# The last graph of a two-layer graph network emitted by halves of its nodes

## The chip, the cores and the metric

The kernel runs on one core of one Trainium2 chip. The metric is the device time of one execution in microseconds (us). A run's time is compared as the median of several executions. The profile is of one further execution; its times are counted from the first instruction (the span), and it has a time of its own.

## What is computed

There are 64 graphs of 256 nodes with 256 features each, and for each a 256x256 adjacency. Layer 0 is a gated recurrent cell over a convolution along the nodes and messages between them; layer 1 is a graph convolution with a residual. Each layer ends in a layer norm. Cut to what matters here:

```python
x_conv = relu(bn(conv1d(relu(bn(conv1d(x, conv1_w))), conv2_w)) + x)    # along the nodes
x_nmp  = (exp(-dist(x @ w_se.T)) * adj) @ relu(x @ w_msg.T + b_msg)
gi, gh = concat(x_conv, x_nmp) @ w_ih.T + b_ih,  x @ w_hh.T + b_hh
r, z   = sigmoid(gi_r + gh_r), sigmoid(gi_z + gh_z)
n      = tanh(gi_n + r * gh_n)
x      = layernorm(x + (1 - z) * n + z * x)
h      = layernorm(x) * ln_gamma + ln_beta
x      = layernorm(x + x + relu((adj @ h) @ W_rel + b_rel + h @ W_root))
```

Layer 0 can be taken graph by graph and node by node once the convolution and the messages are there; layer 1 mixes the nodes of one graph in `adj @ h`.

## The kernel before

**The work.** Graphs are taken in order, `k` = 0 to 63, in eight blocks of eight. A tile of one graph has 128 partitions and two halves: nodes 0 to 127 and 128 to 255 (index `n`). The convolution of the block to come is worked out in small steps, between the parts of the graphs of the present block (`pump`, L940). In the last block there is no convolution to come, so only the graphs' own work is left.

**One graph.** It goes through these functions:

- `gates_rz(k, n)` (L704): for one half, six products of 512 columns into one PSUM bank (L711, L713); VectorE adds the bias (L716) and ScalarE takes the tanh that stands for both sigmoids (L717).
- `gates_n(k, n)` (L719): products for the third gate (L723, L725) and their bias (L726).
- `update(k)` (L733), in three steps. First, for both halves at once: two operations on VectorE into `nn` and its tanh on ScalarE (L739). Second: three operations on VectorE into `w` (L743 and two recorded at the helper's line L103), the statistics of each half (`stats`, L730 and L731), and on GpSimd the two reciprocal roots by a power (L752 to L754) and the shift of the first (L756, L757). Third: `h`, the normalised state, on VectorE (L762), and `X1`, the layer's output, on ScalarE (L765).
- `transposes_h(k)` (L769): `h` is turned by TensorE (L775); ScalarE takes it to `hT` with gamma and beta (L777).
- `project(k)` (L781): for each half two products of 512 columns with `W_rel` and `W_root` side by side (L788); ScalarE copies the first 256 columns to `hr` (L789).
- `aggregate(k)` (L793), in three steps. First: for each half, the adjacency times `hr` is added in PSUM to the root product (L800), and VectorE adds the bias into `y` (L802). Second: relu and residual over both halves (L103), statistics, and the last norm's scale and shift on GpSimd (L810 to L813). Third: ScalarE applies them (L816) and issues the store of both halves (L817).

A product of 512 or of 256 columns is two instructions in the profile, a transpose one: `x8` beside L788 means four products, `x4` beside L775 four transposes.

**The order.** It is written out by hand: each engine runs its instructions in the order in which the program emits them, and waits at the first that is not ready. The loop over `k` (L949 to L990) emits a graph's gates among the second layer of the graph before it: `transposes_h(k - 1)` comes between the gates of the halves, `project(k - 1)` after them, `aggregate(k - 1)` at the end, and the last step of that (the norm's application and the store) after the first gates of the next graph, by `step(y_left)` (L957). After the loop the second layer of graph 63 is emitted alone (L993 to L998): first the last step of graph 62, then graph 63's transposes, projection and aggregation.

**Buffers.** `nn`, `w`, `h`, `hT`, `hr`, `rz` and `gn` have one buffer each, `X1` and `y` two. PSUM's eight banks are handed out in turn. Loads go through SyncE's queue (SP), stores of the output through ScalarE's.

Of the kernel before, what the change touches and what calls it, by code (L numbers as in the profile page):

```python
# [12 lines left out]
F32 = mybir.dt.float32  # L13
AF = mybir.ActivationFunctionType
ALU = mybir.AluOpType

P = 128
B, N, D = 64, 256, 256
C = D // P
TAPS, PAD = 17, 8  # L20
EPS = 1e-5
# [8 lines left out]
BG = 8  # L30
# [45 lines left out]
def gnn_two_layers(  # L76
# [17 lines left out]
    nc = tc.nc  # L94
# [4 lines left out]
    def bank(name):  # L99
        return psum.tile([P, 512], F32, tag="ps", name=name)  # L100

    def stt(o, in0, s, in1, op0=ALU.mult, op1=ALU.add):
        nc.vector.scalar_tensor_tensor(o, in0, s, in1, op0=op0, op1=op1)  # L103
# [25 lines left out]
    mhalf = const.tile([P, 8], F32)  # L129
# [7 lines left out]
    ident = const.tile([P, P], F32)  # L137
# [477 lines left out]
    XG, ADJ, XT, NMP, AT, MSG, X1, H, ST, RZ, OUTS = ({} for _ in range(11))  # L615

    def load(k):

        if k >= B:
            return  # L620
        load_xt(k)
        load_adj(k)
# [9 lines left out]
    def load_x(k):  # L632
        if k < B:
            XG[k] = work.tile([P, C, D], F32, tag="x", name="x")
            nc.sync.dma_start(out=XG[k], in_=x[k].rearrange("(c p) d -> p c d", p=P))
# [51 lines left out]
    def mask(k):  # L687
        nc.vector.tensor_mul(AT[k], AT[k], ADJ[k])

    def passing(k):  # L690
        NMP[k] = work.tile([P, C, N], F32, tag="nmp", name="nmp")
        ps = bank("ps_nmp")
        for d in range(C):
            for m in range(C):
                nc.tensor.matmul(ps[:, d * N:(d + 1) * N], MSG[k][:, m, d * P:(d + 1) * P], AT[k][:, m, :],  # L695
                                 start=(m == 0), stop=(m == C - 1))
        nc.scalar.copy(NMP[k].rearrange("p c n -> p (c n)"), ps)

    def inputs(k, n):
        xc, g = XC[k]  # L700
        q = slice(n * P, (n + 1) * P)
        return q, (xc[:, 0, g, q], xc[:, 1, g, q], NMP[k][:, 0, q], NMP[k][:, 1, q])

    def gates_rz(k, n):  # L704
        if n == 0:
            RZ[k] = (work.tile([P, C, 2 * D], F32, tag="rz", name="rz", bufs=1),
                     work.tile([P, C, 2 * D], F32, tag="gn", name="gn", bufs=1))
        q, ins = inputs(k, n)
        prz = bank("ps_rz")
        for c in range(C):  # L710
            nc.tensor.matmul(prz, XT[k][:, c, q], whh[:, c, 0:2 * D], start=(c == 0), stop=False)  # L711
        for i, t in enumerate(ins):
            nc.tensor.matmul(prz, t, wih[:, i, 0:2 * D], start=False, stop=(i == 3))  # L713
        rz = RZ[k][0]

        nc.vector.tensor_add(rz[:, n, :], prz, brzn[:, :2 * D])  # L716
        nc.scalar.activation(rz[:, n, :], rz[:, n, :], AF.Tanh, scale=0.5)  # L717

    def gates_n(k, n):  # L719
        q, ins = inputs(k, n)  # L720
        pn = bank("ps_n")
        for c in range(C):
            nc.tensor.matmul(pn[:, D:], XT[k][:, c, q], whh[:, c, 2 * D:], start=(c == 0), stop=(c == C - 1))  # L723
        for i, t in enumerate(ins):
            nc.tensor.matmul(pn[:, :D], t, wih[:, i, 2 * D:], start=(i == 0), stop=(i == 3))  # L725
        nc.vector.tensor_add(RZ[k][1][:, n, :], pn, brzn[:, 2 * D:])  # L726

    def stats(mv, k, src):
        st = work.tile([P, 6], F32, tag="bst", name="bst", bufs=4)
        nc.vector.bn_stats(st, src)  # L730
        nc.vector.bn_aggr(mv[:, k, :], st)  # L731
# [37 lines left out]
    def transposes_h(k):  # L769
        hT = work.tile([P, C, N], F32, tag="hT", name="hT", bufs=1)  # L770
        ps = bank("ps_hT")
        for c in range(C):
            for n in range(C):
                q = c * N + n * P
                nc.tensor.transpose(ps[:, q:q + P], H[k][:, n, c * P:(c + 1) * P], ident)  # L775
        for c in range(C):
            nc.scalar.activation(hT[:, c, :], ps[:, c * N:(c + 1) * N], AF.Identity,  # L777
                                 bias=gb[:, 1, c:c + 1], scale=gb[:, 0, c:c + 1])
        H[k] = hT

    def project(k):  # L781
        hT = H[k]
        hr = work.tile([P, C, D], F32, tag="hr", name="hr", bufs=1)
        outs = []
        for n in range(C):
            ps = bank("ps_out")
            for c in range(C):
                nc.tensor.matmul(ps, hT[:, c, n * P:(n + 1) * P], wrr[:, c, :], start=(c == 0), stop=(c == C - 1))  # L788
            nc.scalar.copy(hr[:, n, :], ps[:, :D])  # L789
            outs.append(ps)  # L790
        OUTS[k] = (hr, outs)

    def aggregate(k):  # L793

        hr, outs = OUTS[k]
        y = work.tile([P, C, D], F32, tag="y", name="y")
        for n in range(C):
            po = outs[n][:, D:]
            for m in range(C):
                nc.tensor.matmul(po, ADJ[k][:, m, n * P:(n + 1) * P], hr[:, m, :], start=False, stop=(m == C - 1),  # L800
                                 skip_group_check=True)
            nc.vector.tensor_add(y[:, n, :], po, brel)  # L802
        yield
        stt(y, y, 0.0, X1[k], op0=ALU.max, op1=ALU.add)
        mv = work.tile([P, C, 2], F32, tag="mv", name="mv3", bufs=4)
        for n in range(C):
            stats(mv, n, y[:, n, :])
        q = work.tile([P, C], F32, tag="q3", name="q3", bufs=4)
        sh = work.tile([P, C], F32, tag="sh", name="sh3", bufs=4)
        nc.gpsimd.tensor_scalar(q, mv[:, :, 1], EPS / 4, None, ALU.add)  # L810
        nc.gpsimd.tensor_tensor(q, q, mhalf[:, :C], ALU.pow)
        nc.gpsimd.tensor_mul(sh, mv[:, :, 0], q)
        nc.gpsimd.tensor_scalar(sh, sh, -1.0, None, ALU.mult)  # L813
        yield
        for n in range(C):
            nc.scalar.activation(y[:, n, :], y[:, n, :], AF.Identity, bias=sh[:, n:n + 1], scale=q[:, n:n + 1])  # L816
        nc.scalar.dma_start(out=out[k].rearrange("(c p) d -> p c d", p=P), in_=y)  # L817
        yield


    def step(g):
        if g is not None:
            next(g, None)


    first = conv(0)
    first_pool = ExitStack()
    W2[0] = first_pool.enter_context(tc.tile_pool(name="first", bufs=1)).tile([P, C, NM, D], F32, name="w2all")
    with tc.tile_pool(name="filters", bufs=1, side="right") as filter_pool:
# [47 lines left out]
        brel = const.tile([P, D], F32)  # L877
# [5 lines left out]
        gb = const.tile([P, 2, C], F32)  # L883
# [3 lines left out]
        wrr = const.tile([P, C, 2 * D], F32)  # L887
# [30 lines left out]
    work = ctx.enter_context(tc.tile_pool(name="work", bufs=2))  # L918
# [16 lines left out]
    y_left = None  # L935
    for b in range(NB):
        coming = conv(b + 1) if b + 1 < NB else iter(())
        done, at, goal = 0.0, 0, BG * POINTS - 6

        def pump():  # L940
            nonlocal done, at
            at += 1
            while done < CONV_WEIGHT * at / goal:
                t = next(coming, 1e9)
                if t is None:
                    break
                done += t

        for k in range(b * BG, (b + 1) * BG):  # L949
            load(k + 3)  # L950
            load_x(k + 1)
            up = update(k)
            agg = None
            gates_rz(k, 0)
            pump()
            gates_n(k, 0)
            step(y_left)  # L957
            pump()
            if k > 0:
                transposes_h(k - 1)  # L960
            pump()
            gates_rz(k, 1)
            pump()
            if k + 1 < B:
                passing(k + 1)
            pump()
            if k + 2 < B:
                factors(k + 2)
            gates_n(k, 1)
            pump()  # L970
            if k > 0:
                project(k - 1)
            step(up)
            pump()
            if k + 2 < B:
                distances(k + 2)
            step(up)
            pump()
            if k + 3 < B:
                messages(k + 3)  # L980
            step(up)
            pump()
            if k + 2 < B:
                mask(k + 2)
            if k > 0:
                agg = aggregate(k - 1)
            step(agg)
            step(agg)
            pump()
            y_left = agg  # L990
        for _ in coming:
            pass
    step(y_left)  # L993
    transposes_h(B - 1)
    project(B - 1)
    agg = aggregate(B - 1)
    for _ in range(3):
        step(agg)  # L998

# [40 lines left out]
```

## Time and profile before

| | us |
|---|---|
| median of three runs | 2278.05 (2276.23 to 2279.79) |
| the profiled execution | 2280.43 |
| its span, first to last instruction | 2278.7 |
| TensorE busy in it | 2224.9 |
| VectorE busy | 1678.0 |
| ScalarE busy | 766.9 |
| GpSimd busy | 467.1 |
| mean granted TensorE clock | 0.994 |

In the rows of the timeline the first number is the start in the span and the second the length; a row can hold several instructions in a run, which `x` counts. Square brackets hold the time for which the engine was idle ahead of the row, and what it waited for. Ends of matmuls are modelled. A granted clock of 1.00 is TensorE's full speed. A row can have the line of a helper: all three-operand VectorE work (`stt`) stands at L103, all statistics at L730 and L731.

The tail looks like this. The gates of graph 63 run on TensorE from 2229.70; graph 62's projection starts at 2245.62 and its aggregation at 2249.06, graph 63's transposes at 2255.80, its projection at 2262.45 and its aggregation at 2267.84. The last store is issued at 2275.34.

### The profile page before, as it was taken

The numbers are of one execution on the slowest core, as the hardware profiler recorded it, in microseconds if no ns is written. First come the engines' busy times: TensorE is split into PE (matmuls) and PEld (weight loads), VectorE is DVE, ScalarE is ACT, GpSimd is POOL, SyncE is SP. The second block draws the span as 40 slices with busy tenths as digits, with TensorE's granted clock in tenths as the row PEclk, the third lists the DMA queues.
The fourth block names the chain that finished last, engine by engine and source line by source line (L and its number), as shares of the span: only waits on it lengthen the run. The fifth ranks groups of instructions, "written<-read, shape, count | busy, mean of one in ns | idle before, by whom it ended". The sixth has DMA issues, their size and how long they took to land.

```text
span 2278.7 us, 24459 instructions
## 1 busy us (share of the span) xinstructions
PE 2224.9 (98%) x8386; PEld 1462.9 (64%) x8386; DVE 1678.0 (74%) x3188; ACT 766.9 (34%) x1585; POOL 467.1 (20%) x926
## 2 busy tenths in 40 slices
PE   8999999999999999999999999999999999999996
PEld 5775666666666676656666666666666567666663
DVE  6966889388883998749895698938888398874443
ACT  6433222532234322443224322343223422243332
POOL 0101212122220321223122121222122022122211
PEclk9999999999999999999999999999999999999998
DMA  5931433214422152233422143221442215321100
GB/s 146 314 111 65 139 102 97 97 47 134 139 75 98 57 170 84 75 102 115 140 74 97 62 143 107 95 100 42 139 135 77 98 47 165 98 75 38 46 23 14
DMA packets 212665, 226.68 MB, mean 99 GB/s; under 512 B 22087, under 2 KB 203838, under 8 KB 212542
## 3 DMA queue, kind: packets, MB, share of 16 engines
q1 hardware_dynamic: 189984, 191.14, 26.5%
q10 hardware_dynamic: 22558, 33.99, 4.3%
q8 instruction: 67, 1.10, 0.2%
q14 instruction: 56, 0.46, 0.1%
HBM read 179.22 MB, written 45.88 MB: 99 GB/s over the span
## 4 chain that ended last, share of the span: by engine, by line
PE 76%; DVE 17%; issue 2%; DMA 2%; POOL 1%; ACT 1%; ACTq 0%; SPq 0%; POOLq 0%; DVEq 0%
PE ps_rz L713 16%; PE ps_k L384 10%; PE ps_n L725 8%; PE ps_rz L711 8%; PE ps_out L788 7%; DVE XF L103 6%; PE ps_c L465 5%; PE ps_nmp L695 4%; PE ps_n L723 4%; PE ps_out L800 4%; PE ps_msg L645 4%; DVE w L103 1%; DMA w<-w2m 1%; DVE XF L361 1%; DVE bst L730 1%
## 5 line engine op out<-in xcount | busy, mean ns | idle before, releaser
L103 DVE SCALAR_TENSOR_TENSOR XF<-XF 128x512 f32<-128x512 f32 (+2 forms) x800 | 507.4, 664 | 7.4
L752 POOL TENSOR_SCALAR q<-mv 128x2 f32<-128x2 f32 x64 | 32.1, 501 | 1468.8 <-DVE mv L731 1468.8
L384 PE MATMUL ps_k<-w,XF 128*128 128x256 f32 x1316 | 300.2, 384 | 14.0 <-ACT AT L685 11.6
L384 PEld LDWEIGHTS ps_k<-w,XF 128*128 128x128 f32 x1316 | 247.5, 191 | 61.5 <-ACT AT L685 17.3
L726 DVE TENSOR_TENSOR gn<-ps_n,brzn 128x512 f32<-128x512 f32 x128 | 87.9, 687 | 238.8 <-PE ps_n L725 238.8
L717 ACT ACTIVATE rz<-rz 128x512 f32<-128x512 f32 x128 | 80.6, 630 | 510.7 <-DVE rz L716 510.7
L711 PE MATMUL ps_rz<-whh,xT 128*128 128x512 f32 x512 | 241.8, 595 | 0.0
L713 PE MATMUL ps_rz<-wih,nmp 128*128 128x512 f32 x512 | 240.6, 592 | 0.0
L713 PE MATMUL ps_rz<-wih,xc 128*128 128x512 f32 x512 | 240.6, 592 | 0.0
L788 PE MATMUL ps_out<-wrr,hT 128*128 128x512 f32 x512 | 232.1, 596 | 5.5 <-ACT hT L777 5.5
L716 DVE TENSOR_TENSOR rz<-ps_rz,brzn 128x512 f32<-128x512 f32 x128 | 87.0, 680 | 190.9 <-PE ps_rz L713 190.9
L713 PEld LDWEIGHTS ps_rz<-wih,nmp 128*128 128x128 f32 x512 | 97.3, 190 | 122.4 <-issue 122.4
L713 PEld LDWEIGHTS ps_rz<-wih,xc 128*128 128x128 f32 x512 | 97.3, 190 | 122.4 <-issue 122.2
L788 PEld LDWEIGHTS ps_out<-wrr,hT 128*128 128x128 f32 x512 | 98.0, 192 | 104.7 <-issue 89.1
L656 ACT ACTIVATE msg<-msg 128x512 f32<-128x512 f32 x61 | 38.4, 630 | 332.8 <-DVE msg L654 332.8
L645 PE MATMUL ps_msg<-wms,xT 128*128 128x260 f32 x512 | 131.8, 395 | 4.6 <-DVE XF L400 4.6
L711 PEld LDWEIGHTS ps_rz<-whh,xT 128*128 128x128 f32 x512 | 92.7, 191 | 65.3 <-issue 61.8
L723 PE MATMUL ps_n<-whh,xT 128*128 128x256 f32 x512 | 131.6, 379 | 0.0
L725 PE MATMUL ps_n<-wih,nmp 128*128 128x256 f32 x512 | 131.4, 379 | 0.0
L725 PE MATMUL ps_n<-wih,xc 128*128 128x256 f32 x512 | 131.4, 379 | 0.0
L361 DVE TENSOR_TENSOR XF<-XF 128x512 f32<-128x512 f32 (+3 forms) x128 | 125.2, 1003 | 1.7
L789 ACT COPY hr<-ps_out 128x256 f32<-128x256 f32 x128 | 47.6, 372 | 232.8 <-PE ps_out L788 232.8
(117 smaller groups left out, 3560.5 us busy)
## 6 DMA issues: line engine op xcount, KB each, us to landing
w<-w2m SPq DMA_DIRECT2D x105, 768.0 KB, 5.8
xn<-in_x_dram SPq DMA_DIRECT2D x32, 512.0 KB, 4.4
xt<-xTc ACTq DMA_DIRECT2D x32, 512.0 KB, 3.3
xT<-xt SPq DMA_DIRECT2D x64, 256.0 KB, 3.0
xb<-in_x_dram SPq DMA_DIRECT2D x32, 512.0 KB, 5.9
adj<-in_adjT_dram SPq DMA_DIRECT2D x64, 256.0 KB, 2.8
x<-in_x_dram SPq DMA_DIRECT2D x64, 256.0 KB, 3.0
out_dram<-y ACTq DMA_DIRECT2D x64, 256.0 KB, 2.2
```

The costliest lines, as they stand in the source:

```text
L103: nc.vector.scalar_tensor_tensor(o, in0, s, in1, op0=op0, op1=op1)
L361: (nc.vector.tensor_add if add else nc.vector.tensor_sub)(sl(o, n), sl(a, n), sl(b, n))
L384: nc.tensor.matmul(ps, X[:, slot, c * P:(c + 1) * P], w(m, c), start=(c == 0), stop=(c == C - 1))
L465: nc.tensor.matmul(pss[o], w1[:, c, o * P:(o + 1) * P], xTc[:, c, :], start=(c == 0), stop=(c == C - 1))
L645: nc.tensor.matmul(ps[:, :D + 4], XT[k][:, c, m * P:(m + 1) * P], wms[:, c, :], start=(c == 0), stop=(c == C - 1 and not idle))
L695: nc.tensor.matmul(ps[:, d * N:(d + 1) * N], MSG[k][:, m, d * P:(d + 1) * P], AT[k][:, m, :], start=(m == 0), stop=(m == C - 1))
L711: nc.tensor.matmul(prz, XT[k][:, c, q], whh[:, c, 0:2 * D], start=(c == 0), stop=False)
L713: nc.tensor.matmul(prz, t, wih[:, i, 0:2 * D], start=False, stop=(i == 3))
L723: nc.tensor.matmul(pn[:, D:], XT[k][:, c, q], whh[:, c, 2 * D:], start=(c == 0), stop=(c == C - 1))
L725: nc.tensor.matmul(pn[:, :D], t, wih[:, i, 2 * D:], start=(i == 0), stop=(i == 3))
L788: nc.tensor.matmul(ps, hT[:, c, n * P:(n + 1) * P], wrr[:, c, :], start=(c == 0), stop=(c == C - 1))
L800: nc.tensor.matmul(po, ADJ[k][:, m, n * P:(n + 1) * P], hr[:, m, :], start=False, stop=(m == C - 1), skip_group_check=True)
```

## The change

The loop leaves out graph 63, and a new function `last_graph` emits it. It has the gates of graph 63 and the second layer of graph 62 in it, and everything of graph 63 from `update` on is done for one half at a time, with the halves' steps placed among the steps of graph 62. Graph 62's own second layer keeps its functions. The aggregation of graph 63 runs over `m` (the half that is summed over) in the outer loop and over the output half `n` in the inner one; before, it was the other way round. The last norm is done per half, and each half has its own store: half 0 through SP's queue and half 1 through ScalarE's. All buffers keep their tags and counts, but for the statistics of the last norm, which have a small tag of their own. Instruction shapes become 128x256 (VectorE, ScalarE) and 128x128 (the copies to `hT`), and the GpSimd steps are taken per half on columns of one.

```diff
+    def last_graph(y_before, k):
...
+        def scales(mv, columns):
+
+            q = work.tile([P, 2], F32, tag="q", name="qh", bufs=4)
+            for i, (f, e) in enumerate(columns):
+                nc.gpsimd.tensor_scalar(q[:, i:i + 1], mv[:, 1:2], f, e, ALU.mult, ALU.add)
+            nc.gpsimd.tensor_tensor(q[:, :len(columns)], q[:, :len(columns)], mhalf[:, :len(columns)], ALU.pow)
+            return q
+
+        def shift(mv, q):
+            sh = work.tile([P, 1], F32, tag="sh", name="shh", bufs=4)
+            nc.gpsimd.tensor_mul(sh, mv[:, 0:1], q[:, 0:1])
+            nc.gpsimd.tensor_scalar(sh, sh, -1.0, None, ALU.mult)
+            return sh
+
+        def half(n):
+            rz, gn = RZ[k]
+            a, c = nn[:, n, :], w[:, n, :]
+            stt(a, rz[:, n, :D], 1.0, gn[:, n, D:], op0=ALU.add, op1=ALU.mult)
+            stt(a, a, 0.5, gn[:, n, :D])
+            nc.scalar.activation(a, a, AF.Tanh)
+            yield
+            nc.vector.tensor_sub(c, XG[k][:, n, :], a)
+            stt(c, rz[:, n, D:], 3.0, c, op0=ALU.add, op1=ALU.mult)
+            stt(c, a, 4.0, c)
+            mv = work.tile([P, 1, 2], F32, tag="mv", name="mvh", bufs=4)
+            stats(mv, 0, c)
+            mv = mv[:, 0, :]
+            q = scales(mv, [(1.0, 4 * EPS), (1 + EPS, 4 * EPS * EPS)])
+            nc.vector.tensor_scalar(H[k][:, n, :], c, mv[:, 0:1], q[:, 1:2], ALU.subtract, ALU.mult)
+            sh = shift(mv, q)
+            nc.scalar.activation(X1[k][:, n, :], c, AF.Identity, bias=sh, scale=q[:, 0:1])
+            yield
+
+        def turn_half(n):
+            ps = bank("ps_hT")
+            for c in range(C):
+                nc.tensor.transpose(ps[:, c * P:(c + 1) * P], H[k][:, n, c * P:(c + 1) * P], ident)
+            for c in range(C):
+                nc.scalar.activation(hT[:, c, n * P:(n + 1) * P], ps[:, c * P:(c + 1) * P], AF.Identity,
+                                     bias=gb[:, 1, c:c + 1], scale=gb[:, 0, c:c + 1])
+
+        def project_half(n):
+            ps = bank("ps_out")
+            for c in range(C):
+                nc.tensor.matmul(ps, hT[:, c, n * P:(n + 1) * P], wrr[:, c, :], start=(c == 0), stop=(c == C - 1))
+            nc.scalar.copy(hr[:, n, :], ps[:, :D])
+            outs.append(ps)
+
+        halves_ = [half(n) for n in range(C)]
+        gates_rz(k, 0)
+        gates_n(k, 0)
+        step(y_before)
+        transposes_h(k - 1)
+        step(halves_[0])
+        gates_rz(k, 1)
+        step(halves_[0])
+        gates_n(k, 1)
+        turn_half(0)
+        step(halves_[1])
+        project(k - 1)
+        project_half(0)
+        agg = aggregate(k - 1)
+        step(agg)
+        step(halves_[1])
+        turn_half(1)
+        step(agg)
+        project_half(1)
+        for m in range(C):
+            for n in range(C):
+                nc.tensor.matmul(outs[n][:, D:], ADJ[k][:, m, n * P:(n + 1) * P], hr[:, m, :], start=False,
+                                 stop=(m == C - 1), skip_group_check=True)
+        step(agg)
+        for n in range(C):
+            o = y[:, n, :]
+            nc.vector.tensor_add(o, outs[n][:, D:], brel)
+            stt(o, o, 0.0, X1[k][:, n, :], op0=ALU.max, op1=ALU.add)
+            mv = work.tile([P, 1, 2], F32, tag="mv3", name="mvy", bufs=4)
+            stats(mv, 0, o)
+            q = scales(mv[:, 0, :], [(1.0, EPS / 4)])
+            sh = shift(mv[:, 0, :], q)
+            nc.scalar.activation(o, o, AF.Identity, bias=sh, scale=q[:, 0:1])
+            (nc.sync, nc.scalar)[n].dma_start(out=out[k, n * P:(n + 1) * P, :], in_=o)
...
-        for k in range(b * BG, (b + 1) * BG):
+        for k in range(b * BG, min((b + 1) * BG, B - 1)):
...
-    step(y_left)
-    transposes_h(B - 1)
-    project(B - 1)
-    agg = aggregate(B - 1)
-    for _ in range(3):
-        step(agg)
+    last_graph(y_left, B - 1)
```

More of the change, by code (lines that the diff above doesn't have):

```diff
@@ L823, in step @@
             next(g, None)
+    def last_graph(y_before, k):
+        nn, w, y = (work.tile([P, C, D], F32, tag=t, name=t, bufs=b) for t, b in (("nn", 1), ("w", 1), ("y", 2)))
+        H[k] = work.tile([P, C, D], F32, tag="h", name="h", bufs=1)
+        X1[k] = work.tile([P, C, D], F32, tag="x1", name="x1", bufs=2)
+        hT = work.tile([P, C, N], F32, tag="hT", name="hT", bufs=1)
+        hr = work.tile([P, C, D], F32, tag="hr", name="hr", bufs=1)
+        outs = []
+        def scales(mv, columns):
[74 more added lines that the diff above has]
+            (nc.sync, nc.scalar)[n].dma_start(out=out[k, n * P:(n + 1) * P, :], in_=o)
```

## The prediction

> **What bounds the kernel now.** I read the page first, for the engine that fills the span:
>
> ```profile
> PE 2224.9 (98%) x8386; PEld 1462.9 (64%) x8386; DVE 1678.0 (74%) x3188; ACT 766.9 (34%) x1585; POOL 467.1 (20%) x926
> ```
>
> TensorE is full for 98% of the span. The change moves nothing until the last graph (graph 63), so its whole effect lies where TensorE is not full: the tail. The timeline of TensorE alone (start, busy us, then in brackets the idle time before and what ended it) shows where:
>
> ```profile
> 2245.62 3.60 PE L788 MATMUL ps_out<-wrr,hT 128*128 128x512 f32 x8
> 2249.06 2.19 PE L800 MATMUL ps_out<-hr,adj 128*128 128x256 f32 x8
> 2255.80 1.14 PE L775 MATMUL ps_hT<-ident,h 128*128 128x128 f32 x4 [4.55 <-DVE h L762]
> 2262.45 5.55 PE L788 MATMUL ps_out<-wrr,hT 128*128 128x512 f32 x8 [5.52 <-ACT hT L777]
> 2267.84 2.19 PE L800 MATMUL ps_out<-hr,adj 128*128 128x256 f32 x8
> ```
>
> The first two rows are graph 62, the last three graph 63. Between them TensorE waits 4.55 us for `h` and 5.52 us for `hT`. The chain of work that ended last shows who fills the waits: `w` and its statistics, the GpSimd scales, `h`, then graph 62's whole second norm, which sits on ScalarE ahead of graph 63's `hT`:
>
> ```profile
> 2249.63 0.54 ACT nn L739
> ...
> 2254.18 1.03 POOL q L754
> ...
> 2260.80 0.59 ACT y L816
> 2261.41 0.38 ACTq L817
> ...
> 2261.84 0.57 ACT hT L777
> ```
>
> Last, the table of stretches, which I cut at the clock's own steps (length, PE busy, ..., and third from the end the granted clock):
>
> ```profile
> 16.85:20.26 3.41, 1.75 (x11) 0.98 (x9) 1.85 (x4) 2.22 (x5) 0.00 (x0) 1.00 0.56 210
> ...
> 201.17:204.58 3.41, 1.34 (x7) 0.84 (x5) 2.36 (x9) 0.63 (x1) 1.47 (x3) 1.00 0.24 77
> 204.58:207.99 3.41, 2.84 (x7) 1.76 (x8) 3.40 (x4) 1.09 (x2) 3.11 (x5) 0.50 0.00 0
> ...
> 2252.57:2255.99 3.42, 0.20 (x1) 0.14 (x1) 1.65 (x7) 0.17 (x1) 1.86 (x5) 1.00 0.00 0
> 2255.99:2259.40 3.41, 0.94 (x4) 0.50 (x3) 2.44 (x7) 0.92 (x2) 0.67 (x2) 0.50 0.00 0
> 2259.40:2262.81 3.41, 0.36 (x1) 0.36 (x2) 0.00 (x0) 2.06 (x4) 0.69 (x3) 0.50 0.14 48
> 2262.81:2266.22 3.41, 3.41 (x5) 1.33 (x5) 0.00 (x0) 0.05 (x1) 0.00 (x0) 0.50 0.09 29
> 2266.22:2269.64 3.42, 3.39 (x12) 1.92 (x11) 0.42 (x1) 0.74 (x2) 0.00 (x0) 1.00 0.00 0
> ```
>
> A stretch with TensorE 39% busy (1.34 of 3.41) is followed by one at clock 0.50; one with 51% (1.75) is not. A full stretch at 0.50 is followed by 1.00. (One other stretch, 1914.66 to 1918.07, was 67% busy by the modelled ends and yet followed by 0.50, so the busy share is not the whole rule.) So a wait costs twice: itself, and the matmuls after it at half rate.
>
> **What the Trainium skill says.** "TensorE: Matmul & The Clock Gate", Part 1: the clock is halved after a slack window of about 3.4 us, restored after a busy one, and the windows run free of the kernel. The trace agrees: its steps are 3.41 us apart; that their phase differs between runs no run here shows yet. "SBUF — State Buffer", section "SBUF: two separate sides": VectorE with two SBUF inputs and GpSimd exclude each other for a whole instruction. The trace fits: the GpSimd multiply at L812 takes 0.19 us at best and 2.24 at worst. "ScalarE: Activation LUTs", section "What ACT_TABLE_LOAD costs", prices an activation at 280 ns plus 0.833 ns per element, 93 more per extra pointer; for 128x256 that gives 586 ns, and L816 takes 592.
>
> **The change, step by step.** All times are the profile's span times with the 2200 dropped where short.
>
> *Up to graph 63's gates nothing moves.* TensorE's order and the other queues are the same to the end of `gates_n(63, 1)`, whose stream ends at 2245.62. SP gets one store at its very end, behind nothing.
>
> *Half 0's state.* Its tanh is through long before, but in VectorE's queue `w` of half 0 comes after the bias add of the second rz product, 43.23 to 43.92. A two-input operation on 128x256 has a row of 419 ns; with the 0.03 us between neighbours 0.45. Three take 1.35, statistics 0.46 + 0.18: 45.94. GpSimd: 0.09 to start, 0.28 + 0.28 for the two scales (L752, L753 start to start), 0.72 for a 128x2 power (L811): 47.31. `h` 47.35 to 47.77 (L762, 409 ns). **A new wait**: half 0's transposes stand ahead of `project(62)` in TensorE's queue, so everything behind, graph 62's 8 + 8 instructions too, waits from 45.62 to 47.90, 2.28 us, which does not exist now. On VectorE the bias add of the second n product queues behind `h` as well, 2.0 us late; its dependants (tanh of half 1, done about 49.8) are covered by the stream below.
>
> *The stream.* Two transposes 0.22, `project(62)` 8 x 0.43 = 3.44 (512-wide instructions start 0.43 apart), `project_half(0)` 4 x 0.43 = 1.72, aggregation of 62 8 x 0.215 = 1.72: end 55.00, in PSUM 0.2 later. ScalarE's `hT` of half 0 is done at about 49.3, under `project(62)`: free; it costs its overhang if that cover were under 1.4 us.
>
> *Half 1's state.* VectorE does graph 62's two bias adds (L802) first; they wait for the aggregation just named, so `w` of half 1 starts only at 55.70. Same work as half 0: h at 59.10, transposes 59.65. TensorE's second wait is 4.65 us: the old one of 4.55 has not gone, it has moved by 3.85 us, and the clock halves in it as now.
>
> *Half 1's turn and projection.* What goes is the 5.52 us wait: graph 62's norm no longer stands ahead of `hT`. ScalarE: shift ready 59.64, X1 0.52, the first 128x128 turn at 60.62. For that size no row exists: bounds 0.27 (a 119x128 copy) and 0.56 (a 128x256 turn); by the ScalarE page about 0.48 less 0.03 for the PSUM source; I take 0.42. The projection is 4 instructions, not 8, at half rate 0.86 each: 60.67 to 64.11. The aggregation with m outermost keeps TensorE busy while `hr` of half 1 is copied: half 0's result after 6 x 0.215 + 0.2, 65.60 (now both stood at 2270.09).
>
> *The end by halves.* Half 0: adds and norm 0.05 + 0.45 + 0.45 + 0.64 to 67.19; GpSimd 0.09 + 0.28 + 0.63 + 0.28 + 0.22. The power on one column is not in the trace: 0.71 for two and 1.02 for four columns give 0.55, bounds 0.19 (a plain operation) and 0.71. Half 1 runs 1.5 behind, and its two-input VectorE steps meet half 0's GpSimd steps: 0 to 0.6, I take 0.45. The last activation ends 71.22, the last store is issued at 71.25 against 75.34: **-4.1**. The store is 128 KB in place of 256; 256 KB move for 0.9 us, so -0.4 (bounds 0 and -0.5). Sum **-4.5 us**. SP's store of half 0 starts 1.4 us earlier and hides.
>
> *The clock.* First, windows of another phase shift both kernels' halved stretches; working them through all phases, before ends 0.3 later than in the profile on average and after about as much: nothing. Second, the new 2.28 us wait can itself halve the clock. Taking 45% busy as the limit (between 39 and 51), a window must hold 1.88 us of it: 3.41 - 2.28 + 2 x 0.40 = 1.93 of 3.41 phases, 57%. The price is one window at half rate over the stream, 3.4/2 = 1.7 to 1.8 us. A median over runs mixes phases: 0.57 x 1.8 = **+1.0**. Net **-3.5 us**.
>
> Against the profiled execution (2280.43 us, of which 2278.7 span) that is 2276.9. The runs shown have a median 2.4 us lower, which no step here touches: 2278.05 - 3.5 = **2274.5**. A measurement of this kernel tells about 0.2%, 4.6 us, from no change.
>
> **The rivals.** (1) *The forecast*, 2274.5, own range 2273.0 to 2276.2: the two results without and with the extra halving are -4.5 and -2.7, and phases spread them. For it: every duration has a row. (2) *The first wait rarely halves the clock* and the clock is back before the last aggregation: -4.5 to -5.3, 2273.1. For it: 51% and even 60% busy stretches stay at full clock; against it: the wait leaves as little as 33%. (3) *The pieces give nothing*: GpSimd and ScalarE handle two halves as slowly as one whole, so the powers, the collisions and the store take back 0.3 + 0.2 + 0.4 and the extra halving comes always: -4.5 + 1.8 + 0.9 = -1.8, 2276.3. Against it: only one of the terms is without a near row. (4) *Slower*: the clock halves at the first wait and stays so. The stream of 6.9 us then takes 13.8, and the last aggregation 1.3 more: -4.5 + 8.2 = +3.7, 2281.7, and with the upper bounds above (1.0 together) 2282.7. The place is the wait at 2245.6; it decides if more than two windows after it stay halved (4.5/1.7). For it: the stretches at 0.50 in the profile last up to 10 us. Against it: a full window ended each.
>
> **How the numbers follow.** (1) 0.60, of which 0.07 under 2273.5; (2) 0.22; (3) 0.12; (4) 0.06, half of it past 0.2%. Faster by over 0.2%: 0.29; within: 0.68; slower: 0.03. The range 2272.4 to 2277.6 leaves out (4) and about half of the outer edges of (2) and (3).
>
> **What would show it.** TensorE idle about 2.3 us before half 0's transposes and about 4.6 before half 1's; no 5.5 us wait for `hT`; `w` of half 1 right after graph 62's second bias add; the last store issued 2.5 to 4.5 us earlier; a halved window just after 2247 to 2250 in some executions. Wrong if the first wait is under 1 us, if half 1's `w` starts before graph 62's aggregation ends, or if something ahead of graph 63 moves.

## The result and the profile after

| | before | changed |
|---|---|---|
| first comparison, median of 6 runs each | 2279.36 us (2276.23 to 2285.44) | 2278.66 us (2276.35 to 2282.12) |
| ratio, 95% interval | | 0.9992 (0.9975 to 1.001) |
| later comparison, median of 25 and 21 runs | 2279.88 us (2276.22 to 2284.90) | 2277.83 us (2273.88 to 2287.43) |
| ratio, 95% interval | | 0.9990 (0.9982 to 0.9998) |
| profiled execution, its span | 2280.43, 2278.7 | 2278.09, 2276.3 |

By the later comparison the changed kernel is faster by about 0.1%, 2.3 us, in an interval of 0.5 to 4.1 us, which only just leaves out a difference of nothing; the interval of the first comparison includes it. The forecast was -3.5 us, a ratio of 0.9985, which lies inside both intervals. In absolute time the first median, 2278.66, stood 1.1 above the forecast range's upper end, but before's own median had come out 1.3 higher in that comparison than the 2278.05 from which the forecast counted.

The first line of the changed kernel's page hardly differs. TensorE has the same 8386 instructions, and the other engines do the same work in a few more, smaller ones:

```profile
PE 2224.9 (98%) x8386; PEld 1462.4 (64%) x8386; DVE 1679.6 (74%) x3194; ACT 766.7 (34%) x1588; POOL 470.1 (21%) x935
```

TensorE's part of the timeline (start, length, and in brackets the idle time before and what ended it) answers to the five rows of before:

```profile
2244.70 1.03 PE L725 MATMUL ps_n<-wih,nmp 128*128 128x256 f32 x4
2247.72 0.41 PE L870 MATMUL ps_hT<-ident,h 128*128 128x128 f32 x2 [1.99 <-DVE h L862]
2247.96 3.60 PE L788 MATMUL ps_out<-wrr,hT 128*128 128x512 f32 x8
2252.17 1.98 PE L878 MATMUL ps_out<-wrr,hT 128*128 128x512 f32 x4 [0.61 <-ACT hT L872]
2253.99 1.89 PE L800 MATMUL ps_out<-hr,adj 128*128 128x256 f32 x8
2260.28 0.41 PE L870 MATMUL ps_hT<-ident,h 128*128 128x128 f32 x2 [4.39 <-DVE h L862]
2261.84 3.78 PE L878 MATMUL ps_out<-wrr,hT 128*128 128x512 f32 x4 [1.16 <-ACT hT L872]
2265.42 2.88 PE L903 MATMUL ps_out<-hr,adj 128*128 128x256 f32 x8
```

The first row is the last of graph 63's gates. Its four instructions start 0.215 us apart, so the stream of gates ends at 2244.70 + 0.86 = 2245.56 (in the kernel before, the next row starts 0.86 after the same one, at 2245.62). The two streams end within 0.06 us of each other, so the two spans differ by the tail alone. Two waits of 4.55 and 5.52 us have become four, of 1.99, 0.61, 4.39 and 1.16. Below, **the tail** is the time from the end of that stream to the end of the span: 33.0 us before (2278.66 - 2245.62), 30.75 now. The difference is 2.3 us, the size that the runs show; that the two agree to a tenth is partly chance, since they are two single executions, each with the halved stretches of the clock where they happened to fall.

ScalarE's and GpSimd's rows tell where two of the four waits come from:

```profile
2247.48 0.23 POOL L845 TENSOR_SCALAR shh<-shh 128x1 f32<-128x1 f32 x1
2247.49 0.69 DVE L726 TENSOR_TENSOR gn<-ps_n,brzn 128x512 f32<-128x512 f32 x1
...
2251.66 0.81 ACT L872 ACTIVATE hT<-ps_hT,gb 128x128 f32<-128x128 f32 x2 [3.32 <-PE ps_out L788]
2252.36 0.41 ACT L853 ACTIVATE nn<-nn 128x256 f32<-128x256 f32 x1
...
2255.99 0.42 DVE L802 TENSOR_TENSOR y<-ps_out,brel 128x256 f32<-128x256 f32 x1 [0.51 <-PE ps_out L800]
2256.33 0.41 DVE L855 TENSOR_TENSOR w<-x,nn 128x256 f32<-128x256 f32 x1
...
2260.03 0.78 POOL L845 TENSOR_SCALAR shh<-shh 128x1 f32<-128x1 f32 x1
2260.04 0.68 DVE L103 SCALAR_TENSOR_TENSOR y<-y,x 128x512 f32<-128x512 f32 x1
...
2260.84 0.60 ACT L864 ACTIVATE x<-w,shh,qh 128x256 f32<-128x256 f32 x1 [4.50 <-POOL shh L845]
2261.35 0.79 ACT L872 ACTIVATE hT<-ps_hT,gb 128x128 f32<-128x128 f32 x2
...
2273.49 0.35 ACTq L915 DMA_DIRECT2D out_dram<-y  x1
```

In the row at 2251.66, half 0's turn waits for `ps_out L788`, graph 62's projection, although its own transposes were done 3.5 us before. `hT` has one buffer: it still held graph 62's, which that projection was reading. In the pair from 2255.99, `w` of half 1 starts when graph 62's second bias add has ended, as forecast. In the pair from 2260.03 GpSimd's last shift step and a VectorE operation with two SBUF inputs (`y` and `x`) start within 0.01 us, and the step takes 0.78. The first pair shows the same step of half 0: it takes 0.23, beside a VectorE operation that starts as close but has one input in PSUM. `X1` waits for the longer step, and half 1's `hT` stands behind `X1`.

The last store is issued 27.9 us after the end of the gates, 29.7 before: 1.8 us earlier, less than the 2.5 to 4.5 that the prediction named as a sign.

### The profile page after: what moved, and what is told of

Its sections match the earlier page's. It is cut to its first block, busy times and chain, and to the rows that moved or that the text cites. A ratio compares the mean times of both kernels' runs of the same rounds, so it can differ in the third digit from the quotient of the medians.

```text
span 2276.3 us, 24486 instructions
## 1 busy us (share of the span) xinstructions
PE 2224.9 (98%) x8386; PEld 1462.4 (64%) x8386; DVE 1679.6 (74%) x3194; ACT 766.7 (34%) x1588; POOL 470.1 (21%) x935
## 4 chain that ended last, share of the span: by engine, by line
PE 77%; DVE 15%; DMA 2%; issue 2%; POOL 1%; ACT 1%; SPq 0%; ACTq 0%; POOLq 0%; DVEq 0%
PE ps_rz L713 16%; PE ps_k L384 11%; PE ps_rz L711 8%; PE ps_n L725 8%; PE ps_out L788 6%; DVE XF L103 5%; PE ps_c L465 5%; PE ps_nmp L695 4%; PE ps_n L723 4%; PE ps_msg L645 4%; PE ps_out L800 4%; DMA w<-w2m 2%; PE ps_w L229 2%; DVE w L103 1%; DVE bst L730 1%
## 5 line engine op out<-in xcount | busy, mean ns | idle before, releaser
L788 PE MATMUL ps_out<-wrr,hT 128*128 128x512 f32 x504 | 226.6, 592 | 0.0
L788 PEld LDWEIGHTS ps_out<-wrr,hT 128*128 128x128 f32 x504 | 95.7, 190 | 96.2 <-issue 86.3
L465 PE MATMUL ps_c<-xTc,w 128*128 128x512 f32 x256 | 117.0, 600 | 6.1 <-ACT xTc L457 6.1
```

The costliest lines, as they stand in the source:

```text
L465: nc.tensor.matmul(pss[o], w1[:, c, o * P:(o + 1) * P], xTc[:, c, :], start=(c == 0), stop=(c == C - 1))
```

## The experiments

The first seven kernels below were run once each, so each is judged by the tail of one profile; the one with all the moves has five runs.

**The last norm and the store in two pieces, alone.** The kernel before, with its last aggregation and norm replaced by those of the change:

```diff
-    agg = aggregate(B - 1)
-    for _ in range(3):
-        step(agg)
+    hr, outs = OUTS[B - 1]
+    y = work.tile([P, C, D], F32, tag="y", name="y")
+    for m in range(C):
+        for n in range(C):
+            nc.tensor.matmul(outs[n][:, D:], ADJ[B - 1][:, m, n * P:(n + 1) * P], hr[:, m, :], start=False,
+                             stop=(m == C - 1), skip_group_check=True)
+    for n in range(C):
...
```

> The kernel before, with only the end of the change: graph 63's last aggregation with m outermost, its last norm per half and the store in two pieces, without the interleaving. Theory: from the end of the last projection's stream to the issue of the last store 7.2 us in place of 7.5, from there to the end of the span 2.8 in place of 3.4, together 0.9: tail 32.2 in place of 33.1. Rival (the pieces cost on GpSimd and ScalarE what they give): 33.1 or more.

Its tail is 2277.39 - 2245.22 = 32.2 us, 0.9 under the kernel before:

```profile
2262.06 5.30 PE L788 MATMUL ps_out<-wrr,hT 128*128 128x512 f32 x8 [5.53 <-ACT hT L777]
2267.19 2.19 PE L1000 MATMUL ps_out<-hr,adj 128*128 128x256 f32 x8
...
2274.57 0.35 ACTq L1015 DMA_DIRECT2D out_dram<-y  x1
```

From the last projection's end to the last store's issue it is 7.4 us (7.5 before; 7.2 expected), and from there 2.8 us to the end of the span, 3.3 before (the expectation has 3.4). So the two pieces give 0.6, most of it through the smaller last store. The other 0.3 of the 0.9 isn't theirs: the projection ahead of them, which is the same in both kernels, took 5.30 us here and 5.55 in the profile of before. The granted clock came back 3.3 us after the projection's start here, at 2265.31, and 3.8 us after it before, at 2266.22:

```profile
2261.89:2265.31 3.42, 3.25 (x4) 1.51 (x5) 0.00 (x0) 0.57 (x2) 0.00 (x0) 0.50 0.23 77
2265.31:2268.72 3.41, 3.38 (x11) 1.78 (x10) 0.00 (x0) 0.74 (x2) 0.00 (x0) 1.00 0.00 0
```

(The columns are the stretch, its length, PE busy, ..., and third from the end the granted clock.) That the tail met the expected 32.2 is thus luck in part. The interleaving, with the rest of the 2.3, gives some 1.7 on top in these executions.

**A buffer of its own for hT.**

```diff
-        hT = work.tile([P, C, N], F32, tag="hT", name="hT", bufs=1)
+        hT = work.tile([P, C, N], F32, tag="adj", name="hT", bufs=5)
```

> The changed kernel, with graph 63's hT in a buffer of the adjacency's tag, so that it is another one than graph 62's. The tail is counted from the end of graph 63's gates on TensorE to the end of the span: 33.1 us in the kernel before, 30.75 in the changed one. Theory (a missed reuse of the one hT buffer costs the path): half 0's turn on ScalarE starts at about 2248.3 in place of 2251.66, the 0.6 us wait ahead of half 0's projection goes, the aggregation of graph 62 and all behind it come 0.7 earlier, tail 30.0 at the same clock. Rival (the turn was late for another reason, or something later sets the end): turn still at about 2251.6, tail 30.75.

The 0.61 us wait is gone, and yet the tail is 30.77. The rows and the table of stretches show why:

```profile
2248.05 0.41 PE L870 MATMUL ps_hT<-ident,h 128*128 128x128 f32 x2 [1.99 <-DVE h L862]
2248.30 5.29 PE L788 MATMUL ps_out<-wrr,hT 128*128 128x512 f32 x8
2248.58 0.79 ACT L872 ACTIVATE hT<-ps_hT,gb 128x128 f32<-128x128 f32 x2
2253.43 1.88 PE L878 MATMUL ps_out<-wrr,hT 128*128 128x512 f32 x4
```

```profile
2245.80:2249.21 3.41, 1.42 (x7) 0.71 (x6) 1.87 (x6) 1.14 (x3) 1.51 (x5) 1.00 0.00 0
2249.21:2252.63 3.42, 3.42 (x6) 1.34 (x5) 0.28 (x1) 0.94 (x3) 0.00 (x0) 0.51 0.00 0
```

In this execution the first wait fell into one stretch, which was 42% busy, and the next ran at half clock: graph 62's projection took 5.29 us for 3.60. That is the extra halving which the prediction priced at 1.7 us, and it hid what the buffer gave. The turn starts 0.53 us after the transposes' start (3.94 in the changed kernel), and the projection of half 0 has no wait, so the theory's mechanism is seen; its size isn't settled by this run.

**The same with the first wait filled**, by 4 products whose result nobody reads, so that the clock can't fall there:

```diff
+        busy(4)
         turn_half(0)
```

> The changed kernel with graph 63's hT in a buffer of its own and with 4 products that nobody reads in TensorE's first wait, so that the clock cannot halve there. From the start of half 0's transposes to the start of graph 62's aggregation the changed kernel took 6.27 us, and 7.09 with the buffer alone, where the clock halved. Theory (the buffer gives 0.8, and the halving took it back): 5.4 us, tail 29.9 to 30.1. Rival (the buffer gives nothing, ScalarE's queue holds the turn in another way): 6.2 us or more.

```profile
2248.47 0.41 PE L870 MATMUL ps_hT<-ident,h 128*128 128x128 f32 x2 [0.26 <-DVE h L862]
...
2253.87 1.89 PE L800 MATMUL ps_out<-hr,adj 128*128 128x256 f32 x8
```

5.40 us, as the theory said: the buffer gives 0.9 of the changed kernel's 6.27. The tail is 29.2 us, 0.7 better than expected; the last aggregation was back at full clock here (2.23 us), and at half for a part in the changed kernel (2.88).

**TensorE's waits filled** in the changed kernel: 4, 10 and 2 products, in all of the four waits but the one of 0.61 us.

> The changed kernel, with products whose result nobody reads put into TensorE's waits: 4 ahead of half 0's transposes, 10 ahead of half 1's, 2 ahead of half 1's projection. Theory (the halved clock after the second wait is worth 1.7 us in the projection and up to 1.2 in the aggregation): the clock stays at 1.00 to the end, projection 1.7 us in place of 3.6, half 0's last bias add about 2.8 earlier, tail 28.0. Rival (the end is set by VectorE, GpSimd and ScalarE, not by TensorE's rate): tail within 0.4 of 30.75.

```profile
2263.83 1.98 PE L878 MATMUL ps_out<-wrr,hT 128*128 128x512 f32 x4 [0.36 <-ACT hT L872]
2265.66 2.19 PE L911 MATMUL ps_out<-hr,adj 128*128 128x256 f32 x8
```

The projection of half 1 takes 1.98 us where it took 3.78, the last aggregation 2.19 where it took 2.88, and the tail is 28.3 against 28.0 expected. So the halved clock after the second of its long waits costs the changed kernel 2.4 us, as these two executions have it.

**w of half 1 ahead of graph 62's bias adds.**

```diff
-        step(agg)
-        step(halves_[1])
+        step(halves_[1])
+        step(agg)
         turn_half(1)
```

> The changed kernel, with half 1's w, statistics and h ahead of graph 62's two bias adds in VectorE's queue. Theory (the second TensorE wait is one of queue order, and the halved clock after it a consequence): half 1's h is ready before graph 62's aggregation ends, the 4.4 us wait goes, the projection of half 1 starts about 1.6 us after that aggregation and runs at full clock (1.7 us in place of 3.4), tail 30.75 - 7.4 = 23.4. Rival (another wait takes its place: ScalarE's copy of hr for half 0, which waits for graph 62's aggregation to have read the one hr buffer, stands ahead of X1 and hT): the projection starts 3 us or more after the aggregation, the clock still halves, tail 27 to 28. Rival two (halving the work gives nothing): tail 30.75.

```profile
2250.22 0.43 DVE L855 TENSOR_TENSOR w<-x,nn 128x256 f32<-128x256 f32 x1 [3.64 <-ACT nn L853]
...
2254.17 0.41 PE L870 MATMUL ps_hT<-ident,h 128*128 128x128 f32 x2 [0.88 <-DVE h L862]
2255.19 1.98 PE L878 MATMUL ps_out<-wrr,hT 128*128 128x512 f32 x4 [0.60 <-ACT hT L872]
```

The tail is 24.2 us, 6.5 less, from two lines changed in order. The 4.39 us wait has become 0.88, and the clock stays at full to the end of the last aggregation. The rest to the 23.4 expected is, by the rows, the missed buffer again: `w` waits for `nn`, whose tanh stands on ScalarE behind the turn of half 0, and that waits for graph 62's projection. The rival's copy of `hr` does stand ahead of `X1`, but it was over before `h` was there.

**w of half 0 ahead of the second rz bias.** The second `step(halves_[0])` was moved ahead of `gates_rz(k, 1)`.

> The changed kernel, with half 0's w, statistics and h ahead of the bias add of the second rz product in VectorE's queue. Theory (the first TensorE wait is one of queue order): w of half 0 starts at about 2241.9 in place of 2243.8, h 1.9 earlier, the wait ahead of half 0's transposes 0.3 us in place of 2.0; the bias add of the second rz comes 2.6 later, which nothing on the path waits for; tail 30.75 - 1.8 = 28.9 at the same clock. Rival (what follows was waiting for something else): tail within 0.4 of 30.75.

```profile
2246.99 0.44 PE L870 MATMUL ps_hT<-ident,h 128*128 128x128 f32 x2
```

The tail is 28.7 us against 28.9 expected; half 0's transposes start 0.2 us after the gates' stream (2246.99 against 2246.77), 2.16 in the changed kernel.

**X1 after the turn.**

```diff
             nc.vector.tensor_scalar(H[k][:, n, :], c, mv[:, 0:1], q[:, 1:2], ALU.subtract, ALU.mult)
+            yield
             sh = shift(mv, q)
...
         turn_half(1)
+        step(halves_[1])
```

(and likewise for half 0).

> The changed kernel, with each half's X1, and the shift that it needs, emitted after the half's turn, so that ScalarE takes hT first. Theory (graph 62's two-input relu on VectorE held GpSimd's last shift step to 0.78 us in place of 0.23, and that held X1, which stood ahead of hT): half 1's first turn starts about 0.45 us after its transposes start in place of 1.07, projection of half 1 0.65 earlier, tail 30.1 at the same clock. Rival (hT was waiting for TensorE): no change, 30.75.

```profile
2258.22 0.77 POOL L845 TENSOR_SCALAR shh<-shh 128x1 f32<-128x1 f32 x1
2258.23 0.68 DVE L103 SCALAR_TENSOR_TENSOR y<-y,x 128x512 f32<-128x512 f32 x1
2258.46 0.66 PE L871 MATMUL ps_hT<-ident,h 128*128 128x128 f32 x2 [4.39 <-DVE h L862]
...
2259.16 0.81 ACT L873 ACTIVATE hT<-ps_hT,gb 128x128 f32<-128x128 f32 x2 [4.62 <-PE ps_hT L871]
2259.67 3.78 PE L879 MATMUL ps_out<-wrr,hT 128*128 128x512 f32 x4 [0.55 <-ACT hT L873]
```

The collision is still there, 0.77 us, but off the path. From transposes to projection it is 1.21 us in place of 1.56, with transposes that ran at half clock in this execution (0.66 for 0.41). The tail is 30.4, 0.37 less; 0.65 was expected, and the slower transposes account for some 0.25 of the gap.

**All the moves together**, with a buffer of its own for `hr` too:

> The changed kernel with all of these: w of half 0 ahead of the second rz bias, w of half 1 ahead of graph 62's bias adds, X1 after the turns, graph 63's hT and hr in buffers of the adjacency's tag. Theory (the waits in the changed kernel come from queue order and from reused buffers, and with them goes the halved clock): waits of TensorE after the gates 0.3, 0 and 0.6 us, clock 1.00 to the end, tail 19.9 in place of 30.75; time 13 us under the kernel before, 2266, ratio 0.9942. Rival (the chain of VectorE, GpSimd and ScalarE for one half is the bound, whatever the order): tail over 26, ratio over 0.997.

```profile
2245.03 0.44 PE L871 MATMUL ps_hT<-ident,h 128*128 128x128 f32 x2
2245.31 3.60 PE L788 MATMUL ps_out<-wrr,hT 128*128 128x512 f32 x8
2248.74 1.88 PE L879 MATMUL ps_out<-wrr,hT 128*128 128x512 f32 x4
2250.46 1.89 PE L800 MATMUL ps_out<-hr,adj 128*128 128x256 f32 x8
2252.19 0.38 PE L871 MATMUL ps_hT<-ident,h 128*128 128x128 f32 x2
2253.12 1.98 PE L879 MATMUL ps_out<-wrr,hT 128*128 128x512 f32 x4 [0.55 <-ACT hT L873]
2254.94 2.19 PE L906 MATMUL ps_out<-hr,adj 128*128 128x256 f32 x8
```

One wait of 0.55 us is left beside the 0.2 ahead of the first transposes, the clock is full to the end of the last aggregation, and the tail is 20.3 us against 19.9 expected. The median of 5 runs is 2268.20 us against 2279.96 of before beside it, ratio 0.9947 (0.9933 to 0.9960), where 0.9942 was expected. It beats the kernel before, and the slowest of its runs (2270.06) took less than the fastest of the changed kernel in the later comparison (2273.88), with the same work on every engine.

**The changed kernel once more**, in more rounds:

> The changed kernel once more, against the kernel before in more rounds, since the first comparison left 0.9975 to 1.001 and the tails of the two profiles differ by 2.3 us, 0.10%. Theory (the tail is the whole effect): ratio 0.9990 within its interval, tail 30.7 where the clock is not halved by the first wait, 32.4 where it is. Rival (the change also moves something ahead of graph 63): gates of graph 63 or their order differ, ratio off 0.999 by more than the interval.

The ratio is 0.9990 (0.9982 to 0.9998), and the tail of the profile 30.9 us. Nothing ahead of graph 63 has moved in order; but this execution took 2287.43 us, and its gates ended at 2254.75, 9.2 us later than in the first profile. The clock records show 23.9 us at half clock ahead of the tail in it, 13.7 in the first.

## Why the prediction was right, and which terms were off

*The place and the mechanism were right.* The gain is in the tail alone; the first wait (2.16 us from the end of the gates against 2.28), the second wait that had moved and not gone, the 5.52 us wait that went, half 1's `w` straight after graph 62's bias add, and the end of the kernel (5.5 us from half 0's last bias add to the issue of the last store, 5.6 forecast; 2.8 from there to the end, 2.9 forecast) stand in the trace as written. The power on one column took 0.58 us (0.55). From the start of half 1's first 128x128 turn to the start of its projection it was 0.49 us (0.47 forecast: 0.42 for the turn and 0.05 of handover).

*Four terms were off.* Without an extra halving the prediction had -4.5, and that profile has -2.3. (1) "`hT` of half 0 is done at about 49.3, under `project(62)`: free" failed: it missed that `hT` has one buffer, which graph 62's projection reads to its end. This put graph 62's aggregation and all behind it up to 0.8 us late; with a buffer of its own the step took 5.40 for 6.27. (2) "Shift ready 59.64" failed by 0.55, beyond the lateness that it took over: the exclusion of GpSimd by a two-input VectorE operation, which I had cited and priced at the last norm only (where it came, 0.85 for 0.58), also struck here, and `X1` stood on the path. (3) The clock's phases were said to cost both kernels alike. In this execution the last aggregation ran at half clock at first: half 0's result came 2.5 us after the projection's stream, not 1.5. It did so in the other profile of the changed kernel too (aggregation 3.03 us, 2.19 at full clock). The prediction let the clock come back at 64.11, between projection and aggregation, though none of the clock's steps that it had shown (2262.81, 2266.22) falls there. (4) The end after the last store's issue gave 0.1 more than forecast. Together 0.8 + 0.5 + 1.0 - 0.1 is the missing 2.2.

*The extra halving* at the first wait was right in mechanism and price (5.29 for 3.60 us) and isn't settled in frequency. I had taken 57% of executions, from a limit of 45% busy that the later traces don't bear out (last section). Of the five profiles that have this wait unfilled (the changed kernel twice, the own buffer, half 1's `w` first, `X1` late) one shows it. The +1.0 that it put into the forecast was therefore the least certain term, and it stood in for the terms I had missed: that the forecast of -3.5 came within 1.2 us of the measured -2.3 is in part luck.

*The rivals.* Rival 2 (no halving, -4.5 to -5.3) failed on the missed terms: no halving came in either profile of the changed kernel, and the gain was 2.3. Rival 3 had the nearest size (-1.8), for other reasons than it gave: the pieces alone do give 0.6, and the extra halving didn't come always. Rival 4 didn't occur; the one halving at the first wait ended after one window.

## What to carry to other kernels

When a chain is cut into halves and interleaved, follow each half through every queue that it passes: here the 4.4 us wait survived because one half's first operation stood behind another graph's last, and two lines changed in order were worth 6.5 us, nearly three times the whole change. Look at every buffer of the old schedule that held one stage at a time, since overlap can turn each into a wait (here `hT`, 0.8 us). A wait of TensorE has to be counted together with the matmuls behind it: here half clock followed each of the unfilled waits of about 4.5 us, and one of five of 2.0 us.

What stays open is whether halves are needed at all: the kernel before in a better order, but not cut into halves, was not tried.

## What the runs showed of the hardware

**The clock.** Its steps of 3.41 us lie elsewhere on the same instructions in each profile: the first step after the end of graph 63's gates came 0.1 us later in the kernel before, 1.4 and 1.7 in the two profiles of the changed kernel, and 3.4 in the one with `hT` in a buffer of its own. The prediction had left this open. It took 45% busy as the limit under which half clock follows, and the page of the Trainium skill that it names ("TensorE: Matmul & The Clock Gate", the table in Part 1) speaks of an idle window. The runs show neither: half clock followed stretches far from idle, and the busy share of a stretch, by the modelled ends, doesn't decide:

```profile
200.24:203.66 3.42, 1.48 (x7) 0.95 (x5) 2.50 (x9) 0.63 (x1) 1.36 (x3) 1.00 0.29 77
203.66:207.07 3.41, 2.71 (x9) 1.48 (x10) 3.27 (x4) 1.09 (x2) 3.08 (x6) 1.00 0.00 0
...
201.30:204.72 3.42, 1.46 (x6) 0.91 (x7) 2.46 (x6) 1.72 (x3) 3.04 (x6) 1.00 0.00 0
204.72:208.13 3.41, 3.41 (x5) 1.35 (x4) 3.41 (x5) 0.12 (x1) 2.80 (x4) 0.50 0.00 0
...
1642.77:1646.18 3.41, 2.29 (x12) 1.45 (x12) 3.38 (x5) 1.97 (x5) 0.00 (x0) 1.00 0.00 0
1646.18:1649.60 3.42, 3.42 (x10) 2.71 (x9) 3.28 (x8) 0.23 (x1) 0.00 (x0) 0.50 0.02 5
1915.84:1919.25 3.41, 2.29 (x11) 1.68 (x11) 3.38 (x6) 1.83 (x4) 0.00 (x0) 1.00 0.00 0
1919.25:1922.67 3.42, 3.42 (x17) 3.02 (x16) 3.21 (x9) 0.00 (x0) 0.44 (x2) 1.00 0.00 0
```

A stretch that was 43% busy was followed by full clock in the first pair (the last norm in two pieces, alone) and by half clock in the second (`w` of half 0 first). The last two pairs are of the changed kernel: both first stretches were 67% busy, and half clock followed only one of them. Products whose result nobody reads, put into the waits, held the clock and gained 2.4 us without any step moved.

**The spread.** Single executions of one kernel spread over 13 us (2273.88 to 2287.43 in the later comparison), several times the effect under study. The time at half clock in the body of the kernel is one part of that: with 10.2 us of it the gates of graph 63 ended at 2243.0 to 2246.8 in the profiles, with 13.7 at 2245.6 to 2245.9, with 17.1 at 2247.6, with 23.9 at 2254.8. Between the two profiles of the changed kernel it explains at most 5.1 of the 9.2 us (10.2 us more at half rate). Some of these stretches come at seven places, some 272 us apart, where TensorE waits 1.1 us for `AT`, a tile of the messages; the last two pairs above are two of these places. Of the seven, between none and four were followed by half clock in a profile: two in the first one of the changed kernel, four in the second. Why it is more in some executions was not tried, and the rest of the spread stays open.
